# First two quads' edge sums by products with a matrix of the ends, all weights loaded at once, and TensorE's order of the beginning written anew

## The chip, the cores and the metric

The kernel runs on one core of one Trainium2 chip. A core has TensorE (matrix products, its weights loaded by a part shown as PEld), VectorE (DVE), ScalarE (ACT), GpSimd (POOL) and SyncE (SP, which here issues DMAs). The metric is the device time of one execution in microseconds (us).

## The reference, cut to what matters

A stack of four graph layers over x of 128 graphs, 128 nodes, 256 features. Each layer is followed by `x = layernorm(x + layer(x))`. The change touches only the beginning, which is layer 0, an attention along 512 edges with four heads of 64:

```python
Xq = (H @ W_lin.T).reshape(bt, n, h, dh)
Xv = (H @ W_val.T).reshape(bt, n, h, dh)
Qs = Xq[:, src]
Kt = Xq[:, dst]
e = jnp.einsum('behd,hd->beh', jax.nn.leaky_relu(Qs + Kt, LRELU_SLOPE), a)
e = e + jnp.log(A0[src, dst] + EPS)[None, :, None]
e_t = e.transpose(1, 0, 2)
m = jax.ops.segment_max(e_t, src, num_segments=n)
ex = jnp.exp(e_t - m[src])
denom = jax.ops.segment_sum(ex, src, num_segments=n)
attn = ex / denom[src]
Vt = Xv[:, dst].transpose(1, 0, 2, 3)
Y = jax.ops.segment_sum(attn[..., None] * Vt, src, num_segments=n)
...
return Y @ W_out.T
```

Layers 1 to 3 use the adjacency matrix as a dense mixing matrix, between products with weights W1, W2, W3 (layer 1), three matrices W (layer 2), and two matrices with batch norms over all graphs (layer 3).

## The kernel before

The graphs are worked in 32 quads of four (`QB = 4`). A quad goes through stages that are named functions: `values_in` (transposes of its x), `values` (its queries and values, one graph at a time), `gather` (the sums Qs + Kt of its edges, in four chunks of 128 edges, by indirect DMAs of GpSimd that read the queries back from DRAM; the second of each pair adds), `score` (one chunk: leaky relu, product with `a`, sum over the 64 features of a head), `softmax_parts` (scans along the 512 edges sorted by source, one yield after each), `attention`, `scatter` (the attention weights into a dense matrix in DRAM by indirect DMAs, then its load as `ad`), `by_row` and `aggregate` (the dense product with the values), `stage_a` (product with `wo`, residual and layer norm), `mix1`, `first`, `mix2`, `second`, `third` (layer 1), `stage_e` (layer 2), `stage_f` and `hidden` (layer 3's first half). Several quads are in different stages at once.

The body stands under `tc.manual_schedule`: each engine runs its instructions in the order in which the program writes them, and semaphores are put between engines where data or a buffer demands it. So the order of calls in `start()` (L943 to L1131), `iteration_0()` (L891) and `iteration(k)` (L789) is the order in each engine's queue, for the DMA issues on SP's and ScalarE's queues too. An instruction that waits holds up all that stands behind it on its engine.

`start()` prepares what depends on the edges alone: the rank of each edge when sorted by source (L971 to L976), a permutation matrix `perm` (L978), the sorted ends as columns `src_idx` and `dst_idx` (`sorted_columns(0)`, products of `perm` with `ends`, L1002), the sorted sources as a row (L1008), which edges occur more than once (L1021 to L1029), the logarithm of the summed weight (L1030 to L1032) and its sorted column `log_col` with the scatter's index `att_idx` (`sorted_columns(2)`, L1037), and the masks of the scans (L1040 to L1043). It also takes quads 0 and 1 through their scores and quad 0 through to `mix2`, and loads weights.

Quads 0 and 1 are gathered like all others (L1005, L1016), each as eight indirect DMAs; as the buffers of the tag `zs` are three, the other chunks are held in the rooms of weights that are loaded later (`l2w`, `l3w1`, `w2t`) and in `z2`. The gathered edges come sorted, since the index columns are sorted; `score` adds `log_col` behind its last chunk (L349) and `softmax_parts` transposes the scores to rows (L356). The weights `w1`, `w2`, `w3`, `l2w`, the bias and the batch norm vectors are loaded on SP's queue behind `scatter(0)` (L1065 to L1073), `l3w1` and `w2t` later still (L1119, L1120). `perm` lies in the room of `w2_s`, into which `second_sums` (L512) later writes sums of blocks of `w2`. Between, the mixing matrices `wt_t`, `split_t`, `diag_bc` and `ahat_t` are made from the adjacency matrix (L1076 to L1105), with a square root on ScalarE (L1099).

`second` (L520) forms a product of blocks from seven smaller ones (14 calls of `product`); its fifth uses block T2, which `late_sums` (L507) makes on VectorE. Behind its second call `iteration_0` puts `attention(1)` and `scatter(1)`, behind the third `score(2, 0)` and `gather_last(2)`; `score(2, 3)`, which needs the latter, stands behind `second`, ahead of the first half of `third` on VectorE and of the transposes of quad 2's scores on TensorE.

Of the kernel before, what the change touches and what calls it, by code (L numbers as in the profile page):

```python
# [25 lines left out]
def gnn_stack(ctx: ExitStack, tc: tile.TileContext, x, adj, w_qv_t, a, w_out_t, src, dst,  # L26
# [14 lines left out]
    nc = tc.nc  # L41
# [86 lines left out]
    with ExitStack() as phase:  # L128
        cst = phase.enter_context(tc.tile_pool(name="cst", bufs=1))

        class Quad:
            pass
# [109 lines left out]
        def values(k, i, copy=None, queue=None):  # L242
# [11 lines left out]
            if i == QB - 1:  # L254
                spill(k, queue)

        def spill(k, queue=None):
            s = quads[k]
            s.qd = q_dram[k % 4]
            (queue or nc.sync).dma_start(s.qd, s.qt.rearrange("p b d -> p (b d)"))  # L260
# [48 lines left out]
        def gather(k, z=None, chunks=range(NE - 1)):  # L309


            s = quads[k]
            s.z = z or {}
            for c in chunks:
                if c not in s.z:
                    s.z[c] = z_buffer(k, c)
            jobs = [(t, c) for t in range(2) for c in chunks]
            if k == 0:
                jobs = [(0, 0), (0, 1), (1, 0), (0, 2), (1, 1), (0, 3), (1, 2), (1, 3)]
            for t, c in jobs:  # L320
                gather_one(k, t, c)
# [16 lines left out]
        def score(k, c):  # L338
# [9 lines left out]
            if c == NE - 1:  # L348
                nc.vector.tensor_add(s.es, s.es, log_col.unsqueeze(2).to_broadcast([P, NE, R]))  # L349

        def softmax_parts(k):

            s = quads[k]
            pe = ps("pe")
            for c in range(NE):
                nc.tensor.transpose(pe[:R, c * P:(c + 1) * P], s.es[:, c, :], ident)  # L356
# [586 lines left out]
        def start():  # L943
# [25 lines left out]
            nc.vector.scalar_tensor_tensor(adj_idx, ends[:, 0, :], float(N), ends[:, 1, :], op0=ALU.mult, op1=ALU.add)  # L969
            key_row = scratch("key_row")  # L970
# [15 lines left out]
            quads[1].xr = load_x(1)  # L986
            nc.sync.dma_start(att_dram[0][:N * N, :].rearrange("(t s) r -> t (s r)", s=N), zero)
            nc.sync.dma_start(wo, w_out_t.rearrange("(c p) f -> p c f", p=P))
            values_in(0, quads[0].xr, nc.scalar.copy)
            for i in range(QB):  # L990
                values(0, i, nc.scalar.copy, nc.scalar)
            quads[2].xr = load_x(2)

            def sorted_columns(t):
                pc = ps("pcol")[:, :NE * 2].rearrange("p (c t) -> p c t", t=2)
                for c in range(NE):
                    for i in range(NE):
                        nc.tensor.matmul(pc[:, c, :], perm[:, i, c * P:(c + 1) * P], ends[:, t:t + 2, i],
                                         start=(i == 0), stop=(i == NE - 1))
                return pc  # L1000

            pc = sorted_columns(0)  # L1002
            nc.vector.tensor_copy(src_idx, pc[:, :, 0])
            nc.vector.tensor_copy(dst_idx, pc[:, :, 1])
            gather(0, {NE - 1: l2w.rearrange("p k c f -> p (k c f)")[:, :QB * D]}, range(NE))  # L1005
            pr = ps("src_row")
            for c in range(NE):
                nc.tensor.matmul(pr[:R, :], src_wide[:, c, :], perm[:, c, :], start=(c == 0), stop=(c == NE - 1))  # L1008
            src_row = scratch("src_row")
            nc.scalar.copy(src_row[:R, :], pr[:R, :])  # L1010

            values_in(1, quads[1].xr, nc.scalar.copy)
            for i in range(QB):
                values(1, i, nc.scalar.copy, nc.scalar)
            z2 = zpool.tile([P, 2, QB * D], F32, tag="z", name="z_1", bufs=1)
            gather(1, dict(enumerate((z2[:, 0, :], z2[:, 1, :], w2t.rearrange("p c d -> p (c d)"),  # L1016
                                      l3w1.rearrange("p c f -> p (c f)")))), range(NE))
# [18 lines left out]

            pc = sorted_columns(2)  # L1037

# [6 lines left out]
            xg3 = load_x(3, "xg", 1, ws)  # L1045

            for c in range(NE):
                score(0, c)
                if c == 1:
                    nc.vector.tensor_copy(att_idx, pc[:, :, 0])  # L1050
                    nc.vector.tensor_copy(log_col, pc[:, :, 1])
            steps = softmax_parts(0)
            for _ in range(2):
                next(steps)
            values_in(2, quads[2].xr, nc.scalar.copy)
            next(steps)
            values(2, 0, nc.scalar.copy)
            values(2, 1, nc.scalar.copy)
            for _ in steps:
                pass  # L1060
            attention(0)
            for i in (2, 3):
                values(2, i, nc.scalar.copy)
            scatter(0)
            nc.sync.dma_start(w1_sb, w1.rearrange("(c p) f -> p c f", p=P))  # L1065
            nc.sync.dma_start(w2_sb, w2.rearrange("(c p) f -> p c f", p=P))
# [4 lines left out]
            for t, vecs in ((bn1, (l3_b1, l3_g1, l3_be1)), (bn2, (l3_b2, l3_g2, l3_be2))):  # L1071
                for i, ap in enumerate(vecs):
                    nc.sync.dma_start(t[:, i, :], ap.rearrange("(c p) -> p c", p=P))  # L1073
# [35 lines left out]
            for c in range(NE - 1):  # L1109
                score(1, c)  # L1110
# [328 lines left out]
```

## Time and profile before

| What | us |
|---|---|
| median of 4 runs | 3212.78 |
| lowest and highest run | 3209.45, 3216.56 |
| the profiled execution, its own time | 3214.84 |
| its span, first to last instruction | 3213.1 |
| TensorE busy | 3130.8 (97%) |
| VectorE busy | 2147.1 (67%) |
| ScalarE busy | 1277.9 (40%) |
| GpSimd busy | 662.4 (21%) |

The mean granted clock of TensorE is 0.988 of full speed over the span. In a timeline, a row gives the start and the length in us, the engine, the line of the program, the operation, `out<-in` with names of tiles, the shape, and in brackets how long the engine had been idle before and what it had waited for. A row can stand for several instructions (`x32`) that follow one another. An f32 product appears as two MATMUL instructions. Tiles that share a buffer may appear under each other's name (`perm` as `w_s`, as it lies in that room).

### The profile page before, as it was taken

How to read it: one execution, taken by the hardware profiler on the slowest of the kernel's cores; microseconds unless marked ns; L12 is line 12 of the kernel's file. 1: busy time of each engine (PE TensorE's matmuls, PEld its weight loads, DVE VectorE, ACT ScalarE, POOL GpSimd, SP SyncE). 2: the span in 40 equal slices, each digit the busy share in tenths (PEclk: the TensorE clock that was granted, in tenths of full speed). 3: DMA queues.
4: the chain of work that ended last, by engine and by line, in shares of the span. 5: the costliest groups of instructions: out<-in, count | busy, mean ns of one | idle time of the engine just before them, and what ended most of it. 6: DMA issues, size and time to landing. Idle time of an engine off the chain costs nothing. (4 is left out here: it accounts for less than half of the span.)

```text
span 3213.1 us, 41204 instructions
## 1 busy us (share of the span) xinstructions
PE 3130.8 (97%) x15884; PEld 2593.6 (81%) x15884; DVE 2147.1 (67%) x4200; ACT 1277.9 (40%) x2229; POOL 662.4 (21%) x541
## 2 busy tenths in 40 slices
PE   6999999999999999999999999999999999999998
PEld 3788888888888888888888888888888888874444
DVE  6666666666666666666666667666666666437878
ACT  2343333333333333333333333343333333326658
POOL 4202222122112112222122111111222211001135
PEclk7999999999999999999999999999999999999999
DMA  7613333333333223333333333223333331005457
GB/s 216 182 47 99 106 99 105 90 102 106 96 96 101 86 78 99 106 99 106 97 95 106 102 90 105 87 78 94 106 99 106 99 86 53 21 27 188 172 190 275
DMA packets 118756, 344.86 MB, mean 107 GB/s; under 512 B 15008, under 2 KB 51744, under 8 KB 110240
## 3 DMA queue, kind: packets, MB, share of 16 engines
q0 software_dynamic: 45552, 151.55, 19.2%
q1 hardware_dynamic: 70960, 188.71, 16.2%
q8 instruction: 126, 2.06, 0.3%
q10 hardware_dynamic: 2048, 1.97, 0.2%
q14 instruction: 70, 0.57, 0.1%
HBM read 256.20 MB, written 85.98 MB: 106 GB/s over the span
## 5 line engine op out<-in xcount | busy, mean ns | idle before, releaser
L535 PE MATMUL ph<-m,w 128*128 128x256 f32 x2048 | 464.0, 380 | 0.0
L616 PE MATMUL p<-w,h 128*128 128x256 f32 x2048 | 462.3, 379 | 0.0
L616 PEld LDWEIGHTS p<-w,h 128*128 128x128 f32 x2048 | 389.0, 190 | 66.1 <-issue 7.7
L535 PEld LDWEIGHTS ph<-m,w 128*128 128x128 f32 x2048 | 387.4, 190 | 51.5
L329 POOL DMA_INDIRECT zs<-qd,src_idx x123 | 120.1, 976 | 1391.7 <-DVE z L739 771.6
L535 PE MATMUL ph<-m,w_s 128*128 128x256 f32 x1536 | 352.4, 379 | 0.0
L666 PE MATMUL po<-l2w,ms 128*128 128x256 f32 x1536 | 348.1, 380 | 1.2 <-DVE ms L658 1.2
L535 PEld LDWEIGHTS ph<-m,w_s 128*128 128x128 f32 x1536 | 291.8, 190 | 39.7
L666 PEld LDWEIGHTS po<-l2w,ms 128*128 128x128 f32 x1536 | 284.8, 190 | 36.3 <-DVE ms L658 1.5
L329 POOL DMA_INDIRECT zs<-qd,dst_idx x123 | 211.1, 1716 | 247.9 <-DMA zs<-qd,src_idx 235.8
L112 ACT ACTIVATE ln_sd<-ln_mv,eps 128x2 f32<-128x2 f32 x192 | 56.3, 293 | 499.1 <-DVE ln_mv L107 499.1
L548 DVE TENSOR_TENSOR h<-ph,u 128x512 f32<-128x512 f32 x128 | 88.2, 690 | 167.5 <-PE ph L535 114.2
L389 POOL DMA_INDIRECT attd<-at,att_idx x128 | 126.1, 986 | 357.3 <-DMA attd<-at,att_idx 247.7
L542 ACT COPY u<-ph 128x512 f32<-128x512 f32 x128 | 75.0, 586 | 244.2 <-PE ph L535 244.2
L346 DVE TENSOR_TENSOR zs<-zs,a_bc 128x1024 f32<-128x1024 f32 x123 | 150.8, 1226 | 4.2
L347 DVE TENSOR_REDUCE es<-zs 128x16 f32<-128x1024 f32 x123 | 150.0, 1220 | 4.2
L344 DVE SCALAR_TENSOR_TENSOR zs<-zs 128x1024 f32<-128x1024 f32 x123 | 149.7, 1217 | 2.4 <-DMA zs<-qd,dst_idx 2.4
L120 DVE TENSOR_SCALAR xr<-xr,ln_mv,ln_rs 128x256 f32<-128x256 f32 x384 | 144.4, 418 | 7.0
L654 ACT COPY ms<-pm 128x512 f32<-128x512 f32 x128 | 71.2, 580 | 194.4 <-PE pm L652 191.0
L105 DVE BATCH_NORM_STATS2 ln_st<-xr 128x6 f32<-128x256 f32 x384 | 144.2, 418 | 5.5
L477 DVE TENSOR_TENSOR h<-z,adc 128x512 f32<-128x512 f32 x62 | 41.9, 676 | 153.9 <-ACT adc L471 153.8
L640 POOL TENSOR_TENSOR xb<-xr,bias 128x512 f32<-128x512 f32 x64 | 81.6, 1275 | 299.8 <-DVE xr L120 161.9
(298 smaller groups left out, 5713.0 us busy)
## 6 DMA issues: line engine op xcount, KB each, us to landing
ad<-attd SPq DMA_DIRECT2D x32, 1024.0 KB, 4.7
zd<-z SPq DMA_DIRECT2D x31, 1024.0 KB, 7.0
zl<-zd SPq DMA_DIRECT2D x62, 512.0 KB, 3.5
xr<-in_x_dram SPq DMA_DIRECT2D x32, 512.0 KB, 5.8
x3d<-xr SPq DMA_DIRECT2D x32, 512.0 KB, 2.8
x3l<-x3d SPq DMA_DIRECT2D x32, 512.0 KB, 5.1
out_dram<-x3l POOLq DMA_DIRECT2D x31, 512.0 KB, 5.6
qd<-qt SPq DMA_DIRECT2D x30, 512.0 KB, 2.6
```

What stands on the lines that cost most here:

```text
L105: nc.vector.bn_stats(st[:, i, :], r[:, i, :])
L120: nc.vector.tensor_scalar(r[:, i, :], r[:, i, :], mv[:, i, 0:1], rs[:, i:i + 1], op0=ALU.subtract, op1=ALU.mult)
L329: nc.gpsimd.indirect_dma_start(out=s.z[c], out_offset=None, in_=s.qd, in_offset=bass.IndirectOffsetOnAxis(ap=idx[:, c:c + 1], axis=0), com ...
L344: nc.vector.scalar_tensor_tensor(z, z, SLOPE, z, op0=ALU.mult, op1=ALU.max)
L346: nc.vector.tensor_mul(z3, z3, a_bc.unsqueeze(1).to_broadcast([P, QB, D]))
L347: nc.vector.reduce_sum(s.es[:, c, :], z.rearrange("p (r d) -> p r d", d=DH), axis=AX.X)
L389: nc.gpsimd.indirect_dma_start(out=ad, out_offset=bass.IndirectOffsetOnAxis(ap=att_idx[:, c:c + 1], axis=0), in_=s.at[:, c, :], in_offset= ...
L535: nc.tensor.matmul(bank[g][:, i].rearrange("p b n -> p (b n)"), wa[:, c, f:f + P], s.m2[:, blk_b, c].rearrange("p b n -> p (b n)"), start= ...
L548: nc.vector.tensor_add(block(g, row, col), bank[g], kept_[g])
L616: nc.tensor.matmul(p3[:, t * D:(t + 1) * D], s.h2[f // 2][:, f % 2, j + t, :], w3_sb[:, f, :], start=(f == 0), stop=(f == K2 - 1))
L640: nc.gpsimd.tensor_add(s.xb[:, j:j + 2, :], xj, bias.unsqueeze(1).to_broadcast([P, 2, D]))
L666: nc.tensor.matmul(po[:, i % 2, :], mss[i][:, t, dc, :], l2w[:, t, dc, :], start=(n3 == 0), stop=(n3 == 3 * DC - 1))
```

## The change

Edge sums of quads 0 and 1: a matrix `onehot` (nodes by 512 edges, unsorted) has a one at each edge's source and one more at its target. `ends_sum(k, h)` multiplies it with the queries of two of the quad's graphs, four products of 128x512 for the four chunks of edges, and ScalarE copies each result to the chunk's buffer. The sixteen gathers of these quads and their two spills of queries to DRAM go. Since the edges are then in the order of the input, `score` adds the weight's logarithm from the unsorted column `ends[:, 3, :]` in each chunk, and `sorted_scores` multiplies the scores with `perm`, which sorts and transposes them at once; `softmax_parts` uses that bank where it is there.

Loads: all weights, both zero fills of the scatter's DRAM and the x of quads 2 and 3 are issued on SP's queue right behind the x of quad 1.

Order: `sorted_columns(0)`, now used only from quad 2 on, moves behind `ahat_t`; the work on duplicates and the logarithm comes ahead of quad 1's `values`; the parts of quads 1, 2 and 3 are interleaved anew with the scores; `score(1, 3)` moves ahead of `stage_a(0)`; `sorted_scores(1)` and the softmax of quad 1 come behind two `first`; `second_sums` moves behind the last `mix2`.

```diff
-            if i == QB - 1:
-                spill(k, queue)
+            if i == QB - 1 and k > 1:
+                spill(k)
...
+        def ends_sum(k, h, onehot):
+            s = quads[k]
+            for c in range(NE):
+                pz = ps("pz")
+                nc.tensor.matmul(pz, onehot[:, c * P:(c + 1) * P], s.qt[:, 2 * h:2 * h + 2, :], start=True, stop=True)
+                nc.scalar.copy(s.z[c][:, h * 512:(h + 1) * 512], pz)
+
+        def sorted_scores(k, perm, chunks=range(NE)):
+            s = quads[k]
+            if 0 in chunks:
+                s.pe = ps("pe")
+            for c in chunks:
+                nc.tensor.matmul(s.pe[:R, :], s.es[:, c, :], perm[:, c, :], start=(c == 0), stop=(c == NE - 1))
...
-            if c == NE - 1:
+            if weight is not None:
+                nc.vector.tensor_scalar(s.es[:, c, :], s.es[:, c, :], weight[:, c:c + 1], None, op0=ALU.add)
+            elif c == NE - 1:
...
+            onehot = scratch("onehot")
+            nc.vector.tensor_scalar(onehot, rows_i[0], pos_col[:, 0:1], None, op0=ALU.is_equal)
+            nc.vector.scalar_tensor_tensor(onehot, rows_i[1], pos_col[:, 0:1], onehot, op0=ALU.is_equal, op1=ALU.add)
...
             values_in(0, quads[0].xr, nc.scalar.copy)
-            for i in range(QB):
-                values(0, i, nc.scalar.copy, nc.scalar)
...
+            z_room(0)
+            for h in range(2):
+                for i in range(2):
+                    values(0, 2 * h + i, nc.scalar.copy)
+                ends_sum(0, h, onehot)
...
+            pr = ps("src_row")
...
             pc = sorted_columns(2)
+            values_in(1, quads[1].xr, nc.scalar.copy)
+            for c in range(2):
+                score(0, c, ends[:, 3, :])
+                values(1, c, nc.scalar.copy)
+            nc.vector.tensor_copy(att_idx, pc[:, :, 0])
+            nc.vector.tensor_copy(log_col, pc[:, :, 1])
...
+            for c in range(2, NE):
+                score(0, c, ends[:, 3, :])
+            sorted_scores(0, perm, range(NE - 1))
+            values(1, 2, nc.scalar.copy)
+            sorted_scores(0, perm, (NE - 1,))
+            values(1, 3, nc.scalar.copy)
             steps = softmax_parts(0)
-            for _ in range(2):
+            for _ in range(3):
                 next(steps)
...
+            z_room(1)
+            ends_sum(1, 0, onehot)
...
             nc.vector.tensor_copy(diag_bc, pr)
+            for _ in steps:
+                pass
+            attention(0)
+            scatter(0)
+            ends_sum(1, 1, onehot)
             nc.vector.tensor_add(an, a_sb, ident)
...
-            values_in(3, xg3, nc.scalar.copy)
-            gather(2)
-            for c in range(NE - 1):
-                score(1, c)
+            pc = sorted_columns(0)
+            nc.vector.tensor_copy(src_idx, pc[:, :, 0])
+            nc.vector.tensor_copy(dst_idx, pc[:, :, 1])
+            values_in(2, quads[2].xr, nc.scalar.copy)
+            for c in range(3):
+                score(1, c, ends[:, 3, :])
+            for i in range(QB):
+                values(2, i, nc.scalar.copy)
+            values_in(3, quads[3].xg, nc.scalar.copy)
+            quads[4].xg = load_x(4, "xg", 1, ws)
             for j in range(QB):
                 by_row(0, j, nc.vector.tensor_copy if j % 2 else None)
             aggregate(0)
+            score(1, 3, ends[:, 3, :])
+            gather(2)
             stage_a(0)
-            for i in range(QB):
+            for i in range(2):
                 values(3, i, nc.scalar.copy)
-            quads[4].xg = load_x(4, "xg", 1, ws)
-            score(1, NE - 1)
...
             mix1(0, 0)
             mix1(0, 2)
+            for i in range(2, QB):
+                values(3, i, nc.scalar.copy)
+            first(0, 0)
+            first(0, 1)
+            sorted_scores(1, perm)
             steps = softmax_parts(1)
-            first(0, 0)
             next(steps)
-            second_sums()
             for i in range(QB):
-                if i + 1 < QB:
+                if i > 0 and i + 1 < QB:
                     first(0, i + 1)
                 mix2(0, i)
                 next(steps, None)
+            second_sums()
```

## The prediction

> **What bounds the kernel now.** I read the page first: TensorE is busy 97% of 3213.1 us, and slices 2 to 36 stand at 9 tenths. From there on a late start is simply carried to the end, so the change is worth what it moves the moment at which TensorE stops waiting. Then I read stretches of ten us (per engine busy us and instructions, then TensorE's granted clock, DMA share, GB/s):
>
> ```profile
> 20.00:30.00 10.00, 9.76 (x25) 3.65 (x24) 6.20 (x18) 2.94 (x7) 6.71 (x6) 0.85 0.65 174
> 30.00:40.00 10.00, 6.86 (x32) 5.14 (x30) 5.02 (x11) 2.78 (x6) 3.42 (x3) 0.84 0.98 243
> 40.00:50.00 10.00, 1.60 (x8) 1.51 (x8) 9.83 (x11) 0.00 (x0) 7.69 (x7) 0.50 0.86 256
> 50.00:60.00 10.00, 7.80 (x24) 4.35 (x24) 7.59 (x8) 4.03 (x8) 3.86 (x3) 0.64 1.06 201
> 70.00:80.00 10.00, 1.26 (x9) 0.72 (x8) 9.83 (x9) 2.65 (x3) 5.81 (x7) 0.50 0.69 256
> 80.00:90.00 10.00, 9.54 (x47) 7.22 (x48) 4.58 (x13) 1.47 (x3) 3.75 (x3) 0.77 1.03 318
> ```
>
> TensorE is nearly idle in 40 to 50 and 70 to 80, where VectorE computes the scores of quads 0 and 1. The timeline of TensorE (start, duration, idle before) names the gaps; all those after 24 us up to 110 us add up to 0.24+3.14+10.59+0.91+0.67+1.38+8.00+1.20+2.15 = 28.3 us.
>
> ```profile
> 35.62 5.99 PE L998 MATMUL pcol<-ends,w_s 128*128 128x2 f32 x32 [3.14 <-DVE ends L1035]
> 52.20 1.02 PE L356 MATMUL pe<-ident,es 128*16 128x128 f32 x4 [10.59 <-DVE es L349]
> 78.14 1.12 PE L416 MATMUL py<-adc,xv 128*64 128x128 f32 x8 [8.00 <-ACT adc L402]
> 108.40 2.07 PE L498 MATMUL pm<-wt_t,h 128*128 128x128 f32 x8 [2.15 <-ACT h L458]
> ```
>
> After a gap the granted clock is 0.50 for some us, as stretches of one us show (TensorE alone, then clock):
>
> ```profile
> 37.00:38.00 1.00, 1.00 (x6) 0.50 1.00 213
> ...
> 57.00:58.00 1.00, 1.00 (x3) 0.89 1.16 176
> ...
> 109.00:110.00 1.00, 1.00 (x6) 0.50 1.03 348
> ```
>
> VectorE's timeline shows what the change moves: the scores wait for the logarithm, which stands in ScalarE's queue behind quad 1's copies; the second quad's softmax ends just ahead of `second(0)`.
>
> ```profile
> 34.81 0.16 DVE L1032 SCALAR_TENSOR_TENSOR ends<-small,small 128x4 f32<-128x4 f32 x1 [8.31 <-ACT small L1031]
> 37.08 1.21 DVE L344 SCALAR_TENSOR_TENSOR zs<-zs 128x1024 f32<-128x1024 f32 x1
> 53.26 1.21 DVE L358 TENSOR_TENSOR_SCAN f<-reset_f,pe 16x512 f32<-16x512 bf16 x1 [1.11 <-PE pe L356]
> 85.88 0.69 DVE L433 TENSOR_TENSOR xr<-xr,po 128x512 f32<-128x512 f32 x1 [4.95 <-PE po L430]
> ```
>
> **What TensorE gains in work.** An f32 product with 512 columns is a pair of instructions; four `values` (8 products) follow each other at 1.72 us per `values`, so 0.86 us each. Added: 16 edge products (`ends_sum`) 13.8 us and 8 of `sorted_scores` 6.9; removed: two sets of transposes (97.82 to 98.26) 0.9. Net 19.8 us, to be put into 28.3 us of gaps. So the gain is bounded by 8.5 us even if every gap were filled, and is decided by the order.
>
> **What leaves or moves without a price.** Sixteen indirect gathers (GpSimd, 19.4 to 54.5) and two spills go; nobody waits for GpSimd there then. The weight loads on SP's queue (72.45 to 106.3 before) move ahead of everything: 9.1 MB with `xr1`, at the 256 to 318 GB/s of the rows 29 to 36 us, over by about 42. Behind them on SP wait only quad 2's spill (at about 77) and the load of `ad` (about 66), so nothing is late. What they could delay are the four picks from `adj` (5.2 to 7.1 us to landing, the last starts at 12.4): VectorE wants them at 22.2, the logarithm at 25.1. Only beyond 9.8 us would each us cost one.
>
> **The path, stage by stage.** *To the first score.* First `values` ends at 10.2 as before, the second at 11.95; its copy 0.4; four edge products to 15.8; two `values` to 19.25; copy 0.4; four edge products to 23.2; last copy (0.59) 23.8. The matrix of ends costs VectorE two ops of 128x512 (0.42 to 0.69 each, taken 1.3), behind which the ranks move, but `perm` is ready by 14.7 and is used at 23.2: hidden. Table load 1.28 and logarithm 0.20: 25.3; four small ops 0.67: first score at 26.0, before 37.08.
> *Scores of quad 0.* A chunk takes 3.64 (37.08 to 40.72), with its own add of the weight 0.17 more; two small copies 0.15 and the keep and reset masks 1.6 now lie between: 26.0 + 15.25 + 1.75 = 43.0. Last sorted product 0.86: first scan at 44.0, before 53.26, so 9.3 ahead.
> *Softmax to `at`.* Two scans and a subtraction 3.1, to 47.1. Then VectorE's order has `adj_t`, `wt_t`, `diag`, `diag_bc` ahead of the third scan, and TensorE's has `values(1, 3)` and four edge products ahead of the transpose: 44.0 + 1.73 + 3.45 = 49.2; the four steps took 63.92 to 65.91, 2.0: 51.2. Two scans 2.45, transposes 0.5, reciprocal and product 0.8: `at` at 54.9, before 61.30: 6.4 ahead.
> *To the scores of quad 1.* `ends_sum(1, 1)` starts at 54.0 after some 4 us with under 1 us of work. At full clock it ends at 57.4, all at 0.50 at 60.9; the restart at 52.20 took until 57.5 to come back, so I take 59.1. Copy 0.6, table load and root 1.5, two small ops 0.5, transpose 0.4: 62.4 (before the root's table was loaded while ScalarE idled). `sorted_columns(0)`, formerly at 15.2 off this path, took 3.63 at full clock and 5.99 mostly at half; after this gap 5.4: 67.8. So score(1, 0) starts at 68.0, before 68.74: only 0.7 ahead.
> *To `stage_a`.* Three chunks of 3.8 instead of 3.64 to 79.4, two row copies 1.25 to 80.6 (before 80.93). ScalarE's two copies wait behind `values(2)` and the transposes of quad 3 (7.8 us of TensorE from 67.8, 1.5 to 2 more at half clock, then 2.1): 80.9. From there to the first add 4.95 by the row at 0.50; at full clock 0.9+0.6+1.75 = 3.25, but score(1, 3) now stands before it on VectorE until 84.4. Taken 84.9, before 85.88: 1.0 ahead.
> *To `second`.* Product of `stage_a` ends 86.6; two `values` 3.45, two `mix1` 1.8, two `values` 3.45, two `first` 3.45, `sorted_scores(1)` 3.45: 102.2; then three `mix2` and two `first` 6.1 and the last `mix2` behind its relu: first product of `second` at 109.2, before 110.27. Its fifth product needs `late_sums`. VectorE now does `second_sums` (4.9) after the last scan (112.6), so T2 is there at 118.1, while TensorE is ready at 109.2 + 7.5 = 116.7. It waits 1.4; that product started at 118.75 before: 0.65 ahead.
> *Given back.* `late_sums` ends at 118.8, `at` of quad 1 at 119.6, before 116.1: 3.5 late. GpSimd queues four scatters and `gather_last(2)` behind it, whose second transfer goes from 129.90 to 133.4:
>
> ```profile
> 129.90 1.60 POOL L329 DMA_INDIRECT zs<-qd,dst_idx  x1 [3.74 <-DMA zs<-qd,src_idx]
> ...
> 212.50 1.60 POOL L329 DMA_INDIRECT zs<-qd,dst_idx  x1 [3.29 <-DMA zs<-qd,src_idx]
> ```
>
> The later one landed 6.2 after its start (score at 218.68), so 139.6; score(2, 3) 3.8: 143.4. TensorE wants it at 142.92 - 0.65 = 142.3 and waits 1.1. Sum 0.65 - 1.1: 0.4 us later than before. The profiled run took 3214.84 around its span of 3213.1, 2.1 over the median of 3212.78; the same 0.4 on the median gives 3213.2, on the profiled run 3215.2.
>
> [...]
>
> **Rivals.** *The clock stays at 1.00.* For it: the new order leaves gaps of 1 to 3 us where there were 8 and 10. Then `ends_sum(1, 1)` ends 1.7 and `sorted_columns(0)` 3.5 earlier, score(1, 0) at 64.5, the first add at 80.95 (score(1, 3) ends then), T2 at 114.15, and the wait at score(2, 3) stays 1.0: 4 us gained, 3209.2. Against it: the rows at 36 and 108.
> *Half clock from 43 to 84.* The stretches 36.7 to 40.1 and 40.1 to 43.5 would be only 62 to 65% busy (waits for the third and fourth chunk's scores). The rows show the drop at 1.25 us of work in 3.4 and none in full stretches; between lies nothing. If two thirds don't hold it, the last sorted product, `values(1, 3)` and a part of `ends_sum(1, 0)` cost 3.1 more, a late recovery in `values(2)` 1.7, aggregate and `stage_a` 1.5: 3213.2 + 6.3 = 3219.5, slower. It decides from a threshold above two thirds on.
> *Loads in the way.* Picks that land 13 us after their start instead of 7 make everything behind the scores 3 us later: 3216. Against it: DMA share was 0.97 to 1.13 at 9 to 16 us before as well.
>
> **How the numbers follow.** The forecast, no change, gets 0.55, the first rival 0.22, the second 0.18, the third 0.05. A measurement of this kernel can tell about 0.2%, 6.4 us: below 3206.4 is faster, above 3219.2 slower. Each has some 4 us of its own, since the stages' terms are bounded by 1.7 to 3.5. The first rival leaves about half of its 0.22 beyond the lower edge if the wait at score(2, 3) goes too, the forecast 0.08: faster 0.19. The second gives 0.12, the third 0.02, the forecast 0.07: slower 0.21; no change 0.60. Range 3205 to 3221: the first rival less 4, the second plus 1.5.
>
> **What would show it.** First score at 26 and first scan at 44 show the first two stages right; `at` of quad 0 at 55; score(1, 0) at 68 and a clock of 0.50 about 54 to 57 and 64 to 71 show the lead lost to ScalarE's root and the columns; score(1, 0) at 65 speaks for the first rival, a first scan after 46 for the second. A gap of TensorE ahead of the fifth product of `second`, behind `late_sums`, and one ahead of the transposes of quad 2's scores show what is given back. If TensorE has no gap at either place, the sum is wrong by 2.5 us there.

## The result and the profile after

The changed kernel takes 3219.05 us (median of 38 runs, 3217.02 to 3224.95); the kernel before took 3214.13 beside it (58 runs, 3208.53 to 3217.01). Ratio 1.002, 95% interval 1.0016 to 1.0025: some 6 us slower by that ratio, 4.9 by the medians, 6.5 by the means (3220.19 and 3213.68), just at what a measurement of this kernel can tell from no change. The profiled execution took 3223.56 us (span 3221.8, clock 0.990), 8.7 more than the profiled one before; 31 of the 38 runs were faster.

The stretches of ten us after the change (columns as before: busy us and instructions of TensorE, its weight loads, VectorE, ScalarE and GpSimd, then TensorE's clock, DMA share, GB/s):

```profile
20.00:30.00 10.00, 9.78 (x40) 4.75 (x40) 5.63 (x15) 4.85 (x9) 0.00 (x0) 1.00 1.06 402
30.00:40.00 10.00, 10.00 (x30) 5.56 (x30) 9.79 (x15) 2.47 (x6) 0.00 (x0) 0.66 0.41 101
40.00:50.00 10.00, 9.24 (x21) 3.17 (x20) 7.17 (x9) 3.36 (x7) 0.00 (x0) 1.00 0.00 0
50.00:60.00 10.00, 6.51 (x18) 3.10 (x17) 5.15 (x12) 2.92 (x6) 2.48 (x4) 0.72 0.00 1
...
70.00:80.00 10.00, 10.00 (x31) 6.39 (x32) 7.85 (x11) 2.87 (x8) 0.00 (x0) 0.76 0.03 12
80.00:90.00 10.00, 8.21 (x61) 6.24 (x61) 9.76 (x13) 4.96 (x9) 3.47 (x4) 1.00 0.52 176
```

The two holes of TensorE (1.60 and 1.26 busy) are filled. The loads are over before 40 us, when the DMA share falls to nothing. But the clock is still at half in a part of 50 to 80. VectorE's timeline, then GpSimd's second transfer of `gather_last(2)`:

```profile
26.76 1.22 DVE L355 SCALAR_TENSOR_TENSOR zs<-zs 128x1024 f32<-128x1024 f32 x1
...
45.34 1.21 DVE L373 TENSOR_TENSOR_SCAN f<-reset_f,pe 16x512 f32<-16x512 bf16 x1 [1.13 <-PE pe L347]
...
72.09 1.22 DVE L355 SCALAR_TENSOR_TENSOR zs<-zs 128x1024 f32<-128x1024 f32 x1
...
88.80 0.68 DVE L448 TENSOR_TENSOR xr<-xr,po 128x512 f32<-128x512 f32 x1
```

```profile
136.41 1.59 POOL L323 DMA_INDIRECT zs<-qd,dst_idx  x1 [3.36 <-DMA zs<-qd,src_idx]
```

Before, the first score of quad 1, score(1, 0), stood here:

```profile
68.74 1.22 DVE L344 SCALAR_TENSOR_TENSOR z<-z 128x1024 f32<-128x1024 f32 x1
```

The first score comes 10.3 us and the first scan 7.9 us earlier than before (37.08 and 53.26), as the change means them to. Yet score(1, 0) starts at 72.09, 3.35 later, and the first add of `stage_a` 2.9 later (85.88). TensorE's timeline shows where the lead goes:

```profile
55.06 0.60 PE L394 MATMUL pat<-ident,m 16*128 16x16 f32 x4 [2.40 <-DVE m L384]
55.59 6.44 PE L338 MATMUL pz<-qt,pos 128*128 128x512 f32 x8
...
64.83 0.45 PE L1125 MATMUL half_ps<-ident,src_row 128*128 128x128 f32 x1 [2.69 <-DVE src_row L1123]
65.07 6.83 PE L1056 MATMUL pcol<-ends,w_s 128*128 128x2 f32 x32
...
113.25 3.62 PE L550 MATMUL ph<-m,w 128*128 128x256 f32 x16
...
121.89 3.69 PE L550 MATMUL ph<-m,w_s 128*128 128x256 f32 x16 [0.77 <-DVE m L524]
...
147.41 0.60 PE L371 MATMUL pe<-ident,es 128*16 128x128 f32 x4 [1.11 <-DVE es L362]
```

`ends_sum(1, 1)` (6.44 us for eight instructions that take 3.70 at full clock) and the sorted columns (6.83 instead of 3.63) run at half clock behind waits of 2.40 and 2.69 us, the first until 61.14, the second all the time. The last two rows are the waits that the late second softmax causes. The first product of `second` before, then SP's store of quad 1's layer output, before and after:

```profile
110.27 4.40 PE L535 MATMUL ph<-m,w 128*128 128x256 f32 x16
```

```profile
292.82 0.32 SPq L686 DMA_DIRECT2D x3d<-xr  x1
```

```profile
296.28 0.32 SPq L701 DMA_DIRECT2D x3d<-xr  x1
```

`second` starts 3.0 later (113.25 against 110.27). The two waits widen this to 4.5 at the second half of `third` (147.84 against 143.36); by quad 1's layer output it is 3.46. From there the distance hardly changes: 2593 us later, at the last such store, it is 3.73 (2889.11 against 2885.38). The rest of the pair's 8.7, 5.0 us, arises in the last 330 us, where both kernels run the same instructions.

**What the clock does.** In both traces TensorE's clock changes only at points that lie whole multiples of 3.413 us apart, and their place differs from one execution to the next: before, the first change is at 9.44 and the last at 3207.73, 937 times 3.4133 apart. Taken modulo 3.4133, all changes of the execution after lie at 3.11 to 3.14, all before at 2.61 to 2.65, and in the experiments at 0.2 (`before_tail`) to 3.2 (`best2`). Stretches cut at these points (TensorE's busy us and instructions, then its clock), after:

```profile
27.00:30.42 3.42, 3.42 (x29) 1.00 1.09 392
30.42:33.83 3.41, 3.41 (x16) 0.50 0.94 243
...
47.48:50.90 3.42, 3.28 (x9) 1.00 0.00 0
50.90:54.31 3.41, 0.81 (x6) 1.00 0.00 0
54.31:57.72 3.41, 2.66 (x7) 0.50 0.00 0
57.72:61.14 3.42, 3.42 (x5) 0.50 0.02 5
61.14:64.55 3.41, 1.01 (x4) 1.00 0.01 2
64.55:67.96 3.41, 3.13 (x16) 0.50 0.24 48
67.96:71.38 3.42, 3.42 (x18) 0.50 0.62 261
71.38:74.79 3.41, 3.41 (x13) 0.50 0.00 0
74.79:78.20 3.41, 3.41 (x9) 1.00 0.01 2
...
81.62:85.03 3.41, 1.62 (x23) 1.00 0.72 223
85.03:88.44 3.41, 3.41 (x32) 1.00 0.47 175
```

After a stretch with 0.81 or 1.01 us of work the clock is halved, after one with 1.62 it is not; in these rows it comes back after stretches that are full (57.72 to 61.14, 71.38 to 74.79), not after one with 2.66. The sorted columns, products two columns wide, fill most of 27.00 to 30.42 and all of 67.96 to 71.38 by the profile, and yet what follows is what follows a pause: the clock falls after the first and does not come back after the second.

So the same wait can cost nothing or 3 us by where the points lie. In the last phase both kernels have a wait of 3.23 us; TensorE's timeline and the stretch with that wait, before:

```profile
2912.04 1.95 PE L1237 MATMUL y<-t,l3w_s 128*128 128x512 f32 x4 [3.23 <-DVE t L1229]
```

```profile
2907.38:2910.80 3.42, 1.43 (x4) 1.00 0.74 272
2910.80:2914.21 3.41, 2.17 (x5) 1.00 0.45 156
```

and after:

```profile
2915.59 3.75 PE L1266 MATMUL y<-t,l3w_s 128*128 128x512 f32 x4 [3.23 <-DVE t L1258]
```

```profile
2911.28:2914.69 3.41, 1.08 (x3) 1.00 0.65 250
2914.69:2918.10 3.41, 2.51 (x3) 0.50 0.42 154
2918.10:2921.52 3.42, 3.42 (x5) 0.50 0.00 0
```

Before, the points divide the wait so that 1.43 us of work stand in the poorer stretch, and the clock stays; after, 1.08, and two stretches go by at half clock. The distance of the pair grows there from 3.55 (2912.04 and 2915.59) to 6.5 at the second row behind it (2915.55 and 2922.04), which is some 3 of the 5.0 us. Behind it the distance goes up and down with the half clocks of each execution, and stands at 8.6 at the last product (3204.29 and 3212.88).

The traces of the experiments below place these 5.0 us: from the last store of a layer output to the end the profiled execution of the changed kernel takes 332.7 us, the one before 327.8, and those of the five experiments whose last phase is left as it was 327.7, 327.8, 329.7, 327.7 and 327.5 (`root_late`, `sorted_early`, `warm`, `loads_late`, `order_only`). The profiled execution after is the exception, and the 3.7 us of the beginning are what the pair says of the two kernels, as far as one execution of each can say it.

### The profile page after: what moved, and what is told of

Same layout as the page of the kernel before. It is cut to its first block, busy times and chain, and to the rows that moved or that the text cites. A ratio compares the mean times of both kernels' runs of the same rounds, so it can differ in the third digit from the quotient of the medians.

```text
span 3221.8 us, 41283 instructions
## 1 busy us (share of the span) xinstructions
PE 3153.8 (98%) x15924; PEld 2600.8 (81%) x15924; DVE 2149.3 (67%) x4208; ACT 1286.8 (40%) x2245; POOL 639.4 (20%) x525
## 5 line engine op out<-in xcount | busy, mean ns | idle before, releaser
L567 ACT ACTIVATE h<-h 128x512 f32<-128x512 f32 x192 | 121.3, 632 | 48.3 <-DVE h L563 48.3
```

The source lines that it names most:

```text
L567: nc.scalar.activation(h, h if src_ is None else src_, AF.Relu)
```

## The experiments

All edits are to the changed kernel unless it says otherwise; the kernel before ran beside each set (medians 3213.9 to 3214.4). Theory: the lead is lost to half clocks behind TensorE's waits, and some to the waits of the late second softmax. Rival: the 20 us of products that are new on TensorE cost what they last. As an interval here is some 3 us wide to either side, one run alone rarely decides; the traces say where the time goes.

**The root out of the way.** The chain from `an` to `ahat_t` is moved behind `mix1(0, 2)`.

```diff
             ends_sum(1, 1, onehot)
-            nc.vector.tensor_add(an, a_sb, ident)
...
-            nc.vector.tensor_scalar(ahat_t, pr, dinv, None, op0=ALU.mult)
-
             pc = sorted_columns(0)
...
             mix1(0, 2)
+            nc.vector.tensor_add(an, a_sb, ident)
...
+            nc.vector.tensor_scalar(ahat_t, pr, dinv, None, op0=ALU.mult)
```

> The changed kernel with the square root's chain (an to ahat_t) moved behind mix1(0, 2). Theory (the lead is lost between at of quad 0, 56.5 us, and the first score of quad 1, 72.1 us, to ScalarE's root behind its edge copies and to half clock): the first score of quad 1 starts 3 to 5 us earlier, TensorE has no gap of 2.7 us ahead of the sorted columns, and the time falls by 3 to 5 us, ratio to the kernel before 1.0005 to 1.0011 instead of 1.0020. Rival (TensorE's added 19.8 us of products set the time, whatever the order): the score starts earlier, but second starts where it did, ratio 1.0020. Rival (the difference comes from the last 330 us, by the clock): ratio 1.0020 as well.

Measured: median 3216.26, ratio 1.0012 (1.0003 to 1.0021). TensorE's timeline:

```profile
55.44 6.40 PE L338 MATMUL pz<-qt,pos 128*128 128x512 f32 x8
61.67 4.41 PE L1056 MATMUL pcol<-ends,w_s 128*128 128x2 f32 x32
```

The columns follow `ends_sum(1, 1)` at once and take 4.41 instead of 6.83; score(1, 0) starts at 66.27, 5.8 earlier than in the changed kernel. At `second` 3.6 of these are left (109.69), at the layer output of quad 1 3.5 (292.79). So in this trace the root on ScalarE, with the clock behind it, is the whole distance of the pair in the beginning. The score came earlier than the 3 to 5 us expected; the ratio stands just beyond the 1.0005 to 1.0011 expected, and its interval overlaps that of the changed kernel (1.0016 to 1.0025).

**The second softmax earlier.** `sorted_scores(1)` and the softmax ahead of `values(3, 2)`, `second_sums` ahead of the `mix2` loop.

```diff
             mix1(0, 2)
+            sorted_scores(1, perm)
+            steps = softmax_parts(1)
+            next(steps)
             for i in range(2, QB):
                 values(3, i, nc.scalar.copy)
+                next(steps)
             first(0, 0)
             first(0, 1)
-            sorted_scores(1, perm)
-            steps = softmax_parts(1)
-            next(steps)
+            for _ in steps:
+                pass
+            second_sums()
...
                 mix2(0, i)
-                next(steps, None)
-            second_sums()
```

> The changed kernel with sorted_scores(1) and the softmax of quad 1 moved ahead of values(3, 2), and second_sums ahead of the mix2 loop. Theory (given back at the join): VectorE no longer idles 11.4 us ahead of the first scan; T2 is ready before the fifth product, at of quad 1 comes some 5 us earlier, TensorE loses neither 0.77 us ahead of the fifth product nor 1.11 us ahead of the transposes of quad 2's scores: 1.9 us less, ratio 1.0014. Rival (the waits only move to the copies of mix2 or to the relus): ratio 1.0020, with new gaps of TensorE of about 2 us between 100 and 120 us.

Measured: median 3220.27, ratio 1.003 (1.0019 to 1.0041). The two waits are gone, and from the first product of `second` to the second half of `third` it takes 32.41 us (113.78 to 146.19) instead of 34.59. The time doesn't follow. A row of TensorE's timeline, and the stretch ahead of it:

```profile
199.72 4.91 PE L513 MATMUL pm<-wt_t,h 128*128 128x128 f32 x28 [2.24 <-ACT h L493]
```

```profile
196.11:199.52 3.41, 1.37 (x9) 1.00 0.09 35
199.52:202.94 3.42, 3.22 (x15) 0.50 0.31 123
```

The same row of the changed kernel, behind the same wait of 2.24, takes 3.39; there the stretch held 1.47 us of work and the clock stayed. So this execution gains 1.7 us by quad 0's layer output (198.43 against 200.09), with 0.52 of a new wait ahead of `second`, and has lost them by quad 1's (296.65 against 296.28). Neither the 1.0014 of the theory nor the 1.0020 of its rival was met, though the interval holds the latter; what this edit is worth without unread products isn't shown.

**Unread products in two waits.** A helper of products whose result nobody reads; the first lines here serve all later experiments.

```diff
+        def warm(n):
+            t = ps("warm")
+            for _ in range(n):
+                nc.tensor.matmul(t, ones, wqv[:, 0, :], start=True, stop=True)
...
+            warm(3)
             for _ in steps:
                 pass
             attention(0)
...
+            warm(3)
             pr = ps("half_ps")[:, :N]
```

> The changed kernel with twice three products of 128x512 into a bank that nobody reads, 2.6 us each time, in two gaps of TensorE: ahead of attention(0) and ahead of the root's transpose. Theory (half clock costs): ends_sum(1, 1) takes 3.7 us instead of 6.44, the root comes 2.7 us earlier, the columns and values(2) lose less; the time falls by 3 to 6 us, ratio 1.0002 to 1.0011. Rival (the work sets the time): 5 us of products more and no gain, ratio 1.0020 or more.

Measured: median 3217.32, ratio 1.0011 (1.0002 to 1.002). TensorE's timeline:

```profile
54.84 3.70 PE L338 MATMUL pz<-qt,pos 128*128 128x512 f32 x8
...
58.52 2.82 PE L961 MATMUL warm<-wqv,ones 128*128 128x512 f32 x6
61.35 0.30 PE L1132 MATMUL half_ps<-ident,src_row 128*128 128x128 f32 x1
61.48 3.63 PE L1061 MATMUL pcol<-ends,w_s 128*128 128x2 f32 x32
```

Both groups are back at full clock, score(1, 0) is at 65.30 (6.8 earlier than in the changed kernel), `second` at 107.01 (6.2 earlier), quad 1's layer output at 289.91, 2.9 ahead of the kernel before. In this execution, then, the half clocks were the whole of the loss in the beginning. The median, 3.4 over that of the kernel before beside it, doesn't show as much: it falls by 1.7 us, the mean by 3.9 (3216.27), and the interval overlaps that of the changed kernel. Other executions have their points elsewhere and may lose on other waits; that is argued from the points, not shown.

**Loads where they were.** All loads on SP behind the x of quad 2, but for that of quad 3, are put behind `scatter(0)`.

```diff
             quads[2].xr = load_x(2)
-            nc.sync.dma_start(w1_sb, w1.rearrange("(c p) f -> p c f", p=P))
...
             scatter(0)
+            nc.sync.dma_start(w1_sb, w1.rearrange("(c p) f -> p c f", p=P))
...
             ends_sum(1, 1, onehot)
```

> The changed kernel with the weight loads and the second zero fill moved back behind scatter(0) on SP's queue. Theory (the loads cost and bring nothing): ratio 1.0020, within 0.0005. Rival (9 MB at the beginning are in the way of the picks and the first copies): the first score starts 0.5 us or more earlier and the ratio is 1.0015 or less. Rival (loads that come late are waited for): a gap of TensorE ahead of first or of second, ratio 1.003 or more.

Measured: median 3218.06, ratio 1.0016 (1.0007 to 1.0025), first score at 26.09 (26.76), `second` at 113.05. The first score is 0.67 earlier, as the first rival has it, but not the ratio. And the traces have these 0.67 in TensorE's first products: the first two `values` start at 7.04 in both executions and take 4.45 here and 5.12 in the changed kernel, where the record of full clock begins at 9.94; here, counted back from the change at 29.06 in six steps of 3.413 us, it would be 8.58. The interval holds the changed kernel's ratio, and no wait is new: the loads neither cost nor bring what these runs can tell.

**Unread products in every long wait** (fillers), in the kernel before and in the changed one; the diff is of the latter, which also has the two groups of the run above.

```diff
+            warm(2)
             aggregate(0)
...
             aggregate(1)
+            warm(4)
             stage_a(1)
...
+            warm(5)
             attention(2)
...
             for i in range(QB):
+                if i == 1:
+                    warm(2)
                 mix2(1, i)
...
                     product(d.zb, s1, d.t[0], True)
+                    if d.q == 0:
+                        t = ps("warm")
+                        for _ in range(3):
+                            nc.tensor.matmul(t, ones, w2t.rearrange("p c d -> p (c d)")[:, :512], start=True, stop=True)
```

The kernel before has 9 ahead of `aggregate(0)`, and 3 ahead of the sorted columns, 12 ahead of the first softmax, 1 ahead of the root's transpose and 2 ahead of the last `mix2`.

> The kernel before, with 128x512 products whose result nobody reads put ahead of TensorE's long waits of the beginning (3, 12, 1 and 9 of them), of iteration 0 (2, 4, 5 and 2) and of the first quad of the last phase (3). If the clock drops that follow such waits set most of the difference between the kernels: the sorted columns' slow stretches and the 3.9 us stretch after 108.4 go, first product of the second at 106 to 109 instead of 110.27, last x3d load at 2881 to 2884 instead of 2885.4, median 3206 to 3210 against 3213.9. [...]

> The changed kernel with the same unread products, at the same waits where it has them (3 ahead of attention(0), 3 ahead of the root's transpose, 2 ahead of aggregate(0), then as in the run beside it). If the clock drops set most of the difference: sorted columns in about 4 us instead of 6.8, ends_sum(1,1) in 3.7 instead of 6.4, first product of the second at 106 to 109 instead of 113.25, no runs above 3219, median 3208 to 3213, and no more than 3 us over the kernel before with its own fillers. If it is the moved work itself, about 20 us on TensorE between the first softmax and the second: the distance of some 6 us to the kernel before with fillers stays, median 3213 to 3217.

Measured: the kernel before with them 3209.5 (ratio 0.9991, 0.9982 to 1.0), the changed one 3211.54 (0.9994, 0.9985 to 1.0003). Mean clocks of 0.997 and 0.996 over the span. The changed kernel gains 7.5 us of median, the kernel before 4.6; what stands between them falls from 4.9 to 2.0 (means: from 6.5 to 2.6). Each ratio is uncertain by 0.0009, 2.9 us, and the interval of the kernel before with fillers reaches 1.0; the remainder is not told from nothing, nor from half of the 6, and the 6 themselves lie only at the edge. An unread product takes time of its own: by the rows above three of them, six instructions, took 2.82 us at full clock, some 0.9 each. In these two traces `second` starts only 0.85 apart (105.69 and 106.54), and 3.9 more are lost by quad 0's layer output (186.87 and 191.60): 0.78 and 1.01 in the two waits on VectorE, and some 1.7 in a stretch at half clock, 169.4 to 172.8, that the other execution doesn't have. So what is left in this pair is for the most part waits and clock again; all the added products stand ahead of `second`, where the two are 0.85 apart.

**The products of the last phase alone**, in the kernel before (the last part of the diff above).

> The kernel before with the 3 unread products of the last phase's first quad alone, in a wait of 3.2 us there that sometimes brings half a clock behind it. If that drop makes the upper part of the kernel's times: the runs above 3215 go, median 1 to 2 us under the kernel before. If it doesn't: median within 0.5 us of it, with the same spread.

Measured: 3212.22, ratio 0.9999 (0.999 to 1.0008). No run lies above 3215.3, where 5 of the 33 beside it lie above 3216.5, and the median is 1.9 lower; but three runs lie above 3215, where none was expected, the interval holds no change, and eleven runs without one above 3216.5 are no rare thing. Inconclusive.

**Filled, with the second softmax early.** The two edits together, and `warm(2)` behind `second_sums`.

> The changed kernel with the unread products, and with the sorted scores and softmax of quad 1 moved ahead of values(3,2), second_sums ahead of the mix2 loop and two more unread products between them. If what was left between the two kernels with fillers (2 to 3 us in their times, 4.9 in their traces) is the waits of TensorE on the late second scan (0.78 ahead of the fifth product of the second, 1.01 ahead of the transposes of w2t) and a clock drop behind them: neither wait there, first product of the second to the third's second half in 32 to 33 us, x3d load of quad 0 at 187 to 190 instead of 191.6, median 3208 to 3211, level with the kernel before with fillers (3209.5). If it is work: x3d load at 191 to 192, median 3211 to 3213.

Measured: 3209.86, ratio 0.9989 (0.998 to 0.9998), level with the kernel before with fillers. Neither wait is there; from `second` to the second half of `third` 32.31 us (109.60 to 141.91), as in the kernel before with fillers (105.69 to 138.00) and not as in the changed one (34.50). The layer output of quad 0 is missed (192.44), as the columns ran at half clock in this execution, from 63.98 to 70.81, and `second` started 3.1 later.

**The order once more.** What the traces suggest: `ends_sum(1, 1)` as the work of the wait for the first softmax, quad 1's scores right behind, the columns and the root off their path, the second quad's sorted scores ahead of `mix1`, its softmax begun behind them; with the fillers. In the cut diff the root's chain, from `an` to `ahat_t`, stays where it is, and the rest of the beginning moves ahead of it.

```diff
+            ends_sum(1, 1, onehot)
             for _ in steps:
                 pass
             attention(0)
             scatter(0)
-            ends_sum(1, 1, onehot)
+            values_in(2, quads[2].xr, nc.scalar.copy)
+            for c in range(NE):
+                score(1, c, ends[:, 3, :])
...
+            pc = sorted_columns(0)
...
+            warm(5)
+            aggregate(0)
+            gather(2)
+            stage_a(0)
+            for i in range(QB):
+                values(3, i, nc.scalar.copy)
+            sorted_scores(1, perm)
+            mix1(0, 0)
+            mix1(0, 2)
+            steps = softmax_parts(1)
+            next(steps)
+            first(0, 0)
+            next(steps)
             nc.vector.tensor_add(an, a_sb, ident)
...
+            first(0, 1)
+            next(steps)
...
             nc.vector.tensor_scalar(ahat_t, pr, dinv, None, op0=ALU.mult)
...
                 mix2(0, i)
-                next(steps, None)
-            second_sums()
+                if i == 1:
+                    second_sums()
```

> The changed kernel with TensorE's order written once more: ends_sum(1,1) ahead of attention(0), the four scores of quad 1 behind it and ahead of the sorted columns and the root, all of values(3) and then the sorted scores of quad 1 ahead of mix1, the root between the steps of quad 1's softmax, second_sums ahead of the last mix2; and the unread products of the run beside it. If the scan of quad 1 is what orders the beginning: scan at 93 to 98 instead of 106.1, first product of the second at 98 to 103 instead of 113.25, no wait ahead of the fifth product nor of the transposes of w2t, x3d load of quad 1 at 284 to 289 instead of 296.3, median 3203 to 3209. If the TensorE work ahead of iteration 0 fills the time anyway: x3d load of quad 1 no earlier than 291, median 3211 to 3215.

Measured: 3205.43, ratio 0.9979 (0.997 to 0.9988), the spread only 3204.80 to 3208.02: faster than both kernels, and by the medians than both with their fillers too, though there the intervals overlap. Scan of quad 1 at 92.55 (106.08, expected 93 to 98), layer output of quad 1 at 284.30, neither of the two waits. The first product of `second` at 105.21 misses its 98 to 103: `aggregate(0)` comes only at 76.49, as ScalarE's copies of `ad` wait for its load until 74.65, and from there on TensorE works without a wait, 28.7 us as in the changed kernel 29.3 (83.94 to 113.25). What is gained behind it are the two waits that are gone.

**That order without the products.**

> The new order of TensorE's beginning with none of the unread products. If the order itself carries most of that version's gain: no more than 3 us over it, median 3205.5 to 3208.5, and below the kernel before's 3214. If the unread products carry it: 3209 to 3213.

Measured: 3209.34, ratio 0.9989 (0.998 to 0.9998). The median lies in the range of the second expectation, at its lower end, and 0.9 beyond that of the first; yet most of the gain is the order's: by the medians the order alone takes 9.7 us off the changed kernel and brings 4.8 against the kernel before, the products 3.9 more, which the overlapping intervals don't settle. This run answers the rival best: with all the added products and not one unread one its interval lies wholly below that of the changed kernel (1.0016 to 1.0025) and just below 1. So it isn't the added work that made the change slower, but its order. TensorE's timeline shows the wait in which five unread products stood:

```profile
74.77 3.27 PE L431 MATMUL py<-adc,xv 128*64 128x128 f32 x32 [6.07 <-ACT adc L417]
```

**Real work in that wait.** `values(3)` ahead of `aggregate(0)` in place of its five unread products, all four or two (with two unread ones), the sorted scores of quad 1 right behind `stage_a(0)`; the second:

```diff
-            warm(5)
+            for i in range(2):
+                values(3, i, nc.scalar.copy)
+            warm(2)
             aggregate(0)
             gather(2)
             stage_a(0)
-            for i in range(QB):
-                values(3, i, nc.scalar.copy)
             sorted_scores(1, perm)
+            for i in range(2, QB):
+                values(3, i, nc.scalar.copy)
```

> The new order with all of values(3) put into TensorE's wait ahead of aggregate(0), in place of the five unread products there (they ran from 69.8 to 76.5, until adc landed from the DMA), and the sorted scores of quad 1 then right behind stage_a(0). If that wait was real and the scan of quad 1 orders the rest: aggregate still at 76 to 78, scan at 83 to 87 instead of 92.55, first product of the second at 97 to 100 instead of 105.2, x3d load of quad 1 at 277 to 280 instead of 284.3, median 3198 to 3202. If VectorE's norms of stage_a and the scan get into each other's way, or TensorE waits on the norms with nothing to do: first product of the second at 101 to 105, median 3202 to 3206.

> The new order with values(3,0) and values(3,1) and two unread products in TensorE's wait ahead of aggregate(0), in place of the five unread products, and the other two values behind the sorted scores of quad 1, which follow stage_a(0) directly. If ScalarE's copies of the second pair of values held up aggregate(0)'s own copies (2.62 us ahead of the product with wo, where all four were put there): no such wait, scan of quad 1 at 85 to 88, first product of the second at 101 to 104, x3d load of quad 1 at 280 to 283, median 3201 to 3204. If the half clock from 68 to 75 behind the sorted columns stretches whatever stands there: aggregate at 77 to 79, first product of the second at 104 to 106, median 3204 to 3207.

Measured: 3205.04 (ratio 0.9975, 0.9964 to 0.9985) and 3208.7 (0.9982, 0.9973 to 0.9991); not better than the order with five unread products, whose interval both overlap. With all four the scan comes at 92.97, not at 83 to 87, and `second` at 105.69, and the median lies in the second expectation's 3202 to 3206; with two the median is beyond both ranges, though the scan comes at 88.82 and `second` at 104.34. TensorE's and ScalarE's timelines with all four:

```profile
69.89 9.58 PE L251 MATMUL pq<-wqv,xt 128*128 128x512 f32 x16
79.40 1.97 PE L431 MATMUL py<-adc,xv 128*64 128x128 f32 x32
83.99 5.41 PE L445 MATMUL po<-wo,yt 128*128 128x256 f32 x16 [2.62 <-ACT yt L434]
```

```profile
76.81 0.37 ACT L252 COPY qt<-pq 128x256 f32<-128x256 f32 x1 [0.73 <-DMA qd<-qt]
81.42 0.37 ACT L253 COPY xv<-pq 128x256 f32<-128x256 f32 x1 [4.23 <-PE py L431]
```

The copies of quad 3's `values` need the room that `aggregate(0)` is still to read, and hold up ScalarE's copy of its result behind them; with two of them a wait of 2.23 stays at the same place. The expectation that fewer copies would remove it fell.

## Why the prediction was right, and where its sum was not

The forecast, no change at 3213.2, held, and its range holds the 3219.05; but the time lies 5.9 us over the forecast and 0.15 below the bound for slower, where single runs spread over 8 us and the mean, 3220.19, is above that bound. That it counts as no change is luck. The sum of steps foresaw quad 1's layer output 0.4 later; it is 3.5 later.

- **To the first score, first scan, first `at`** (26.0, 44.0, 54.9): 26.76, 45.34, 56.5. Right, each a little short. Of the 0.76 at the first score 0.2 are there at the first copy of queries (10.48, before 10.27) and may have come with the clock, whose record of full speed begins at 9.94 here and at 9.44 before; behind the first score a chunk takes 3.91 instead of 3.81, since the add of the weight takes 0.23.
- **To the scores of quad 1** (68.0): 72.09. Here the sum failed. From `at` on 13.1 us were foreseen and 15.6 taken. The cause was named, half clock behind the wait on the first softmax and behind the root; two terms were mis-sized: `ends_sum(1, 1)`, taken as 5.1, took 6.44, at 0.50 until 61.14, and the columns, taken as 5.4, 6.83, all at 0.50. Between ends of 3.4 and 6.9, and of 3.63 and beyond 5.99, the middle was chosen, where the trace shows the clock at full or at half for whole stretches of 3.413 us. These two are 2.8, small terms give 0.3 back, and with the 1.6 of late start that is the 4.1 by which the step misses.
- **To `stage_a` and `second`** (16.9 and 24.3 us long): 16.7 and 24.5. Right.
- **Given back**: a wait ahead of the fifth product of `second` (1.4) and one ahead of quad 2's transposes (1.1): 0.77 and 1.11, on the engines named. Moving the second softmax removed both.
- **The work on TensorE** (+19.8): busy +23.0, of which some may be products that ran at half clock. It went into the gaps as foreseen; TensorE's idle time is 68.0 us after and 82.3 before.
- **Rivals.** Half clock from 43 to 84 did not come: the stretches from 40.66 to 50.90 are 84 to 96% busy, not 62 to 65, and stay at 1.00. What the clock does behind 62 to 65% could have been looked up in the trace before: the stretch from 2910.80 to 2914.21, shown above, has 2.17 us of work, 63%, and the clock stays at 1.00 behind it; behind 105.02 to 108.43, with 1.26 us, the 1.25 in 3.4 of the prediction, it falls to 0.50. So it was wrong that the rows show nothing between 1.25 us and full stretches, and also that no full one is followed by a drop: 16.27 to 19.68 before is full, mostly of sorted columns, and the clock is at 0.50 from 19.68. Loads in the way: the logarithm was ready at 26.05 for 25.3, and putting the loads back changes nothing. The clock stays at 1.00: made so with unread products, score(1, 0) comes at 65.30, for the 64.5 worked out.
- **Not foreseen**: that the clock's points also decide in the last phase, with 5.0 us between the two profiled executions, and that one execution's sum can thus be off its kernel's median by several us.

What stays open is how the 6.5 us between the means lie in the executions without a trace. The profiled pair shows 3.7 at the last layer output, and the last phases of the other traces suggest that it costs both kernels the same but for chance; then some 3 us are not placed. With every long wait filled 2.6 of the 6.5 are left. The runs don't settle it.

## What to carry to other kernels

TensorE can lose more behind a brief wait than in it (here 2.74 us, 6.44 for 3.70, behind one of 2.40): look at the granted clock behind each of its gaps, and cost what follows in whole stretches, here of 3.413 us, at full or at half, not at something between. Before an operation is moved onto TensorE's free time, see what it will stand behind: a short chain through ScalarE and VectorE ahead of it (here the root, 3 us) delays all of it. And where differences of some us count, one profiled execution isn't enough to place them: the same wait of 3.23 us cost nothing in one and some 3 us in the other.

## What the runs showed of the hardware

In the traces before and after TensorE's clock changed only at points whole multiples of 3.413 us apart, at 2.61 to 2.65 modulo 3.4133 in the one and at 3.11 to 3.14 in the other. Of the stretches between such points, behind the first 10 us and at full clock, those with up to 1.42 us of work (3102.41 to 3105.83, after) were all followed by half clock; with more, both came: it stayed behind 2.16 (2866.40 to 2869.81, before) and fell behind 2.16 (166.38 to 169.79 of `early_fill`). In these two rows of the kernel before the clock falls behind a stretch with 1.74 us of work; behind the one with 1.62 shown above (81.62 to 85.03, after) it stayed:

```profile
3142.88:3146.29 3.41, 1.74 (x10) 1.00 0.97 381
3146.29:3149.71 3.42, 3.42 (x12) 0.50 0.87 315
```

Full clock came back behind a stretch with 2.71 us of work (74.07 to 77.48 of the new order without fillers), and not behind one with 2.87 (3101.92 to 3105.33 before); in the traces before and after it came back behind none with less than 3.31 (3109.24 to 3112.65, after). A gap of 2.24 us was followed by half clock in one execution (`sorted_early`, at 199.52) and not in another (after). Two stretches filled for the most part by products two columns wide were followed by 0.50, though the profile calls the engine busy for 3.42 and 3.41 us of them (27.00 to 30.42 after, 16.27 to 19.68 before). Unread products in the waits took 4.6 us off the median of the kernel before, with an interval that reaches no change (0.9982 to 1.0).
